# Four buffers for the powers of a latent preparation, and a new order for the steps of a cross attention and a router

## The chip, the core and the metric

The kernel runs on one NeuronCore of a Trainium2 chip. The metric is the device time of one execution in microseconds (us), as the median over runs. In the profile PE is TensorE (PEld its weight loads), DVE is VectorE, ACT is ScalarE, POOL is GpSimd and SP is the engine that here only issues transfers. One execution was also taken by the hardware profiler; all durations of single instructions come from it.

## The reference

A decoder of six blocks in float32, for x of 2 x 1024 x 256, each with a layer norm of its input and a residual. What is computed, in short:

```python
x = x + linear_attention_and_ffn(_layernorm(x))          # L0_attn
x = x + latent_attention(ctx, _layernorm(x), mask)       # L0_xattn: q, k rms-normed per head of 64
x = x + gated_cell(_layernorm(x))                        # L0_ffn: a scan of two steps
x = x + causal_attention(_layernorm(x))                  # L1_attn, 16 heads of 16
x = x + cross_attention(_layernorm(x), ctx)              # L1_xattn, 64 context rows
x = x + experts_top2(_layernorm(x))                      # L1_ffn, 8 experts, hidden 1368

def rmsnorm(x, gamma):                                   # of L0_xattn
    norm = jnp.sqrt(jnp.sum(x * x, axis=-1, keepdims=True)) * x.shape[-1] ** (-0.5)
    return x / jnp.maximum(norm, RMS_EPS) * gamma

q = (x @ wq + bq)...; k = (y @ wk + bk)...; v = (y @ wv + bv)...      # L1_xattn
attn = jax.nn.softmax(q @ k.T / 4, axis=-1)
out = (attn @ v) @ wo + bo

logits = x @ router_w                                    # L1_ffn; the two best experts of each token
hidden = gelu(expert_inputs @ w0) * (expert_inputs @ w1)
out = combine(hidden @ wo)
```

## The kernel before

x stays in SBUF as 16 tiles of 128 tokens by 256 features. The blocks run one after the other, each with pools of its own, and in most of them the order of all instructions is the order in which Python records them ("manual schedule"): each engine runs its own queue strictly in that order, and a tile of a pool is handed out again only when all that read its last content have run. A queue whose first instruction waits holds back all behind it.

Three places matter here.

**The preparation of the second batch's latents** (`Latent.prepare(1)`, called from `Latent.run` as `side`, one step between two steps of the first batch's attention). For four pairs of token tiles j it multiplies (`prod`), squares (`square`, ScalarE), keeps the product (`keep`), sums the squares per head (`sums`, VectorE, tile `p_ss` of 128x16) and raises the sums to the power of -1/2 (`inv`, L931, GpSimd, tile `p_ri`). Then come the values, and only then the four `scale` (L937, VectorE) that multiply by `p_ri`; then `qturn` and `kturn` transpose the scaled rows on TensorE (L967). The tiles `p_ss` and `p_ri` have two buffers each (`small`, `bufs=2`). The same steps for the first batch are mixed with the last steps of the block before in `JOINT_ORDER`. In the attention, additions of probabilities (`acc`, L1194) go in turn to VectorE and GpSimd, and the maxima of the scores are reduced by VectorE (`red`, L1065).

**The cross attention** (`Cross`), in four units u of 512 tokens. `CROSS_ORDER` is a list of steps written out; each word names a method and its arguments (`norm_01` is `norm(0, 1)`). For each unit: `stat`, `mean` (VectorE), `root` (a power on GpSimd, L144), `norm` (halves h of two tiles each, VectorE, through `ln_apply`, L183), `turn` (transposes), `xT` (copy from PSUM), `proj` and `q` (query, two halves c), `max` and `red` (a first pass that finds the maxima, reduced by VectorE), `part` (VectorE splits the maxima into three bfloat16 parts), `mT` and `rows` (transposes and copy of these), `sc` and `exp` (scores less the maxima, exponentials), `val`, `sum`, `inv`, `spr`, `os`, `yT` (values, divided by the sums), `out` and `add`. `bias` adds the output's bias row to x (GpSimd, L204). `text`, `keys` and `vals` prepare the context of a batch. The statistics of units 0 and 1 are computed by `stats` at the end of the block before.

Between these steps stand those of the router and the dispatch of the next block: `route_*` (a generator, `Experts.scores`, for one unit: statistics, power, norms, transposes, copy, product with the router, copy), `choose` (top two of a batch, `Experts.choose`), `ones`, `disp` and `put` (rows of the first two experts gathered by matmuls with 0/1 matrices).

PSUM has three tiles of 128x1024 ("s") and two of 128x512 ("t") in this block, so each `max`, `sc` and `spr`, which take two "s" each, waits for what read the tiles before them.

**The first expert** (`Experts.run`). `FIRST_ORDER` lists the steps that mix the first multiplications with the router of the last unit and the choice of the second batch: `up` (both input products of a slice of the hidden layer), `gelu` (ScalarE), `mul` (VectorE). Here PSUM has two "s" tiles.

Of the kernel before, what the change touches and what calls it, by code (L numbers as in the profile page):

```python
# [88 lines left out]
class Core:  # L89
# [3 lines left out]
    def __init__(self, tc):  # L93
        self.tc, self.nc, self.ps, self.tiny = tc, tc.nc, None, None
        self.turn = 0

# [22 lines left out]
    def evac(self, out, in_):  # L119

        self.turn ^= 1
        if self.turn:
            self.nc.vector.tensor_copy(out, in_)
        else:
            self.nc.scalar.copy(out, in_)

# [55 lines left out]
    def ln_apply(self, out, in_, mv, r, i):  # L182
        self.nc.vector.tensor_scalar(  # L183
            out, in_, mv[:, i, 0:1], r[:, i : i + 1], ALU.subtract, ALU.mult
        )

# [458 lines left out]
class Latent:  # L645
# [57 lines left out]
    def small(self, n, name):  # L703
        return self.pool.tile([P, n], F32, tag=name, bufs=2, name=name)
# [217 lines left out]
    def sums(self, b, j):  # L922

        nc = self.k.nc
        ss = self.of["ss", b, j] = self.small(16, "p_ss")
# [3 lines left out]
    def inv(self, b, j):  # L929
        ri = self.of["ri", b, j] = self.small(16, "p_ri")  # L930
# [850 lines left out]

CROSS_ORDER = """
text_0 stat_31 norm_00 norm_01 stat_30 turn_00 bias_0 turn_01 vals_0 text_1 keys_0 xT_0 stat_20 proj_00
vals_1 keys_1 proj_01 norm_11 stat_21 q_00 q_01 norm_10 max_01 mean_3 bias_1 mean_2 turn_11 red_010
turn_10 xT_1 red_011 root_2 proj_11 root_3 norm_21 norm_20 max_00 norm_30 bias_2 norm_31 proj_10 red_001
bias_3 red_000 q_11 q_10 part_0 max_10 turn_30 red_100 turn_31 xT_3 turn_20 red_101 turn_21 max_11 xT_2
mT_0 red_110 rows_0 red_111 sc_00 part_1 exp_00 mT_1 rows_1 sc_01 proj_21 exp_01 proj_20 sc_10 q_20 q_21
val_0 exp_10 max_20 os_0 sum_0 red_200 red_201 sc_11 inv_0 proj_30 exp_11 proj_31 max_21 q_30 q_31 sum_1
red_210 red_211 spr_0 inv_1 val_1 yT_0 part_2 os_1 out_0 spr_1 add_0 mT_2 route_stat_01 rows_2 yT_1
route_stat_00 max_30 route_mean_0 route_root_0 out_1 red_300 route_norm_01 route_norm_00 red_301  # L1790
route_turn_0 add_1 route_xT_0 route_stat_10 max_31 route_stat_11 red_311 route_prod_0 route_mean_1
red_310 route_root_1 route_copy_0 route_norm_11 sc_20 route_norm_10 part_3 route_turn_1 exp_20 mT_3
route_xT_1 sc_21 rows_3 route_prod_1 exp_21 route_copy_1 sc_31 choose_0 choose_0 sum_2 exp_31 choose_0
choose_0 inv_2 spr_2 choose_0 val_2 choose_0 os_2 yT_2 choose_0 sc_30 choose_0 out_2 exp_30 ones_03
ones_02 ones_01 ones_00 disp_00 add_2 route_stat_20 sum_3 put_00 ones_07 ones_06 ones_05 val_3 inv_3
ones_04 spr_3 os_3 route_stat_21 disp_01 yT_3 route_mean_2 put_01 out_3 route_root_2 route_norm_20
route_norm_21 add_3 route_turn_2 route_xT_2 route_prod_2 route_copy_2
# [3 lines left out]
class Cross:  # L1801
# [9 lines left out]
    def __init__(self, k, x, wt, ctxT, const):  # L1811
# [41 lines left out]
        for q in range(4):  # L1853
            part = self.to_rows[q * 32 : q * 32 + 32]
            for sign in (1, -1):
# [9 lines left out]
                for name, shape in (("mv", [P, 4, 2]), ("r", [P, 4]))]  # L1865
# [5 lines left out]
    def stats(self):  # L1871

        k, nc = self.k, self.k.nc
        for u, (mv, r) in self.early.items():
# [7 lines left out]
            yield  # L1882

# [71 lines left out]
    def root(self, u):  # L1955
        self.early[u] = self.of.pop(("mv", u)), self.k.rsqrt(self.of.pop(("ve", u)), 4)

    def norm(self, u, h):
        mv, r = self.early[u]
        xh = self.tile(u, "xh", [P, 4, D])  # L1960
        for i in self.halves(h):
            self.k.ln_apply(xh[:, i, :], self.four(u)[:, i, :], mv, r, i)

    def bias(self, u):
        self.k.add_row(self.four(u), "xb_bo")
# [10 lines left out]
    def xT(self, u):  # L1976
        xT = self.tile(u, "xT", [P, DC, 512])
        self.k.nc.scalar.copy(xT, self.of.pop(("x_s", u)).rearrange("p (c n) -> p c n", c=DC))
# [12 lines left out]
    def q(self, u, c):  # L1991
        k, s = self.k, self.of["q_s", u]
        q = self.tile(u, "q", [P, DC, 512])
        if c == 0:
            k.nc.vector.tensor_scalar(q[:, 0, :], s[:, :512], k.vec("xq_b", 0), 0.25, ALU.add, ALU.mult)
        else:
            k.nc.scalar.activation(q[:, 1, :], s[:, 512:], AF.Identity, bias=self.qb[:, 1:2], scale=0.25)
# [43 lines left out]
    def rows(self, u):  # L2041
        rows = self.tile(u, "mrows", [P, DC, 512], BF16)
        self.k.nc.scalar.copy(rows.rearrange("p c n -> p (c n)"), self.of.pop(("m_t", u)))
# [35 lines left out]
    def os(self, u):  # L2079
        os = self.tile(u, "os", [P, DC, 512])  # L2080
        self.k.nc.scalar.copy(os.rearrange("p c n -> p (c n)"), self.of.pop(("o_s", u)))
# [58 lines left out]
    def run(self, pool, moe):  # L2140
# [3 lines left out]
        nc = self.k.nc  # L2144
# [14 lines left out]
        for step in CROSS_ORDER.split():  # L2159
            name, args = step.rsplit("_", 1)  # L2160
# [7 lines left out]
            else:  # L2168
                getattr(self, name)(*args)

# [3 lines left out]
up_06 route_stat_30 up_08 gelu_06 route_stat_31 route_mean_3 mul_06 route_root_3 gelu_08 mul_08 up_04  # L2174
route_norm_30 route_norm_31 route_turn_3 gelu_04 mul_04 route_xT_3 route_prod_3 up_01 route_copy_3
choose_1 choose_1 choose_1 gelu_01 choose_1 up_00 choose_1 mul_01 choose_1 gelu_00 mul_00 up_0a choose_1
choose_1 up_05 gelu_0a ones_12 ones_13 up_07 gelu_05 ones_10 ones_11 mul_0a gelu_07 disp_10 mul_07
mul_05 up_02 put_10 ones_15 ones_16 ones_14 up_09 gelu_02 ones_17 mul_02 disp_11 gelu_09 mul_09 up_03
put_11 gelu_03 mul_03
# [3 lines left out]
class Experts:  # L2183
# [83 lines left out]
    def scores(self, u, pool, bufs=2):  # L2267
# [15 lines left out]
        yield  # L2283
        for i in range(4):
            k.ln_apply(self.xn[:, 4 * u + i, :], four[:, i, :], mv, r, i)
# [9 lines left out]
        nc.scalar.copy(xT, s.rearrange("p (c n) -> p c n", c=DC))  # L2295
# [533 lines left out]
```

## Time and profile before

| | |
|---|---|
| runs | 1703.24, 1704.68, 1713.89 us; median 1704.68 |
| profiled execution | 1704.63 us, of it 1702.8 us from the first to the last instruction (span) |
| TensorE busy | 1636.1 us, 96% of the span |
| VectorE, ScalarE, GpSimd busy | 809.1, 515.3, 310.3 us |
| mean granted TensorE clock | 0.985 |
| `prepare(1)` | statistics at 282 us, last transposes of the place at issue at 357 us |
| cross attention | from 1101.3 us (first text matmul); last routing product in it ends at 1211.4 us |
| first expert | from 1211.4 us |

All times within the execution count from the span's start. The busy share of an engine is a mean over blocks with different limits, so the prediction reads stretches of the span. "Granted clock" is the share of TensorE's full clock that the chip gave it; at 0.50 a matmul takes twice as long. In lines of the timeline the first number is the start, the second the duration in us, and the square bracket gives the idle time of the engine before it and what ended it.

### The profile page before, as it was taken

To read this page: it belongs to the slowest core of one execution; us is meant where nothing else is said; L and a number is where in the kernel's file an instruction comes from. 1 tells how busy PE (TensorE), PEld (TensorE's weight loads), DVE (VectorE), ACT (ScalarE), POOL (GpSimd) and SP (SyncE) were. 2 spreads that over 40 slices of the span, in tenths; PEclk is the share of its full clock that TensorE was granted. 3 is DMA by queue.
4 is the path that set the end of the run, shared out by engine and by line. 5 is a ranking of instruction groups with operands and counts; after the bars stand their busy time and mean duration, and the time that the engine had idled before them with its cause. 6 is when DMAs were issued, how large, how long until landed. Compare 5 with 4: busy or idle time off the path is not lost.

```text
span 1702.8 us, 21329 instructions
## 1 busy us (share of the span) xinstructions
PE 1636.1 (96%) x8816; PEld 881.5 (52%) x8822; DVE 809.1 (48%) x1458; ACT 515.3 (30%) x870; POOL 310.3 (18%) x376
## 2 busy tenths in 40 slices
PE   7999999989999999999999999889999999999998
PEld 5756544433433447333434433546785665566466
DVE  7714554465545415576667668366531311111322
ACT  2321412323233323245455455433211111111110
POOL 2003301242222202113111012220044000000520
PEclk9999999999999999989999999989899999999999
DMA  6000000000000100000000000170033322232321
GB/s 235 0 1 3 0 0 1 1 1 1 1 1 0 41 0 23 10 2 1 1 2 1 1 1 2 49 228 2 1 114 122 124 86 93 70 124 73 107 64 50
DMA packets 36824, 69.68 MB, mean 41 GB/s; under 512 B 5048, under 2 KB 28152, under 8 KB 36344
## 3 DMA queue, kind: packets, MB, share of 16 engines
q1 hardware_dynamic: 28712, 53.61, 9.4%
q0 software_dynamic: 4608, 11.54, 2.2%
q10 hardware_dynamic: 3408, 3.17, 0.5%
q8 instruction: 70, 1.15, 0.3%
q14 instruction: 26, 0.21, 0.0%
HBM read 54.15 MB, written 14.16 MB: 40 GB/s over the span
## 4 chain that ended last, share of the span: by engine, by line
PE 87%; DVE 9%; ACT 2%; issue 1%; POOL 1%; DMA 0%; SPq 0%; ACTq 0%; POOLq 0%; DVEq 0%
PE ps_s L2556 18%; PE ps_o L2583 9%; PE ps_s L1545 8%; PE ps_o L1585 5%; PE ps_s L1182 4%; PE ps_t L1504 4%; PE ps_s L1055 3%; PE ps_t L570 3%; PE ps_f L587 3%; PE ps_o L1109 3%; PE ps_t L1350 3%; PE ps_s L412 3%; PE ps_t L1620 2%; PE ps_s L904 2%; PE ps_t L1693 1%; DVE part L1561 1%
## 5 line engine op out<-in xcount | busy, mean ns | idle before, releaser
L2556 PE MATMUL ps_s<-xe,w 128*128 128x512 f32 (+1 forms) x528 | 229.0, 592 | 0.0
L1655 ACT ACTIVATE pT<-ps_t 128x512 f32<-128x512 f32 (+3 forms) x344 | 150.7, 490 | 145.3 <-PE ps_t L1620 143.1
L2571 DVE TENSOR_TENSOR hid<-ga,ps_s 128x512 f32<-128x512 f32 (+2 forms) x99 | 62.0, 628 | 268.6 <-ACT ga L2567 268.5
L1545 PE MATMUL ps_s<-kT,qT 32*128 32x512 f32 (+3 forms) x768 | 178.2, 553 | 11.2 <-DVE part L1561 7.2
L1620 PE MATMUL ps_t<-qT,kT 32*128 32x512 f32 (+3 forms) x688 | 182.0, 547 | 2.2 <-ACT pT L1655 2.2
L2556 PEld LDWEIGHTS ps_s<-xe,w 128*128 128x128 f32 (+1 forms) x528 | 98.0, 187 | 121.3 <-issue 120.0
L2583 PE MATMUL ps_o<-wo,hid 128*128 128x256 f32 (+1 forms) x704 | 153.7, 379 | 0.0
L1561 DVE TENSOR_REDUCE part<-ps_s 128x2 f32<-128x1024 f32 (+3 forms) x128 | 130.5, 1024 | 43.6 <-PE ps_t L1620 37.3
L2583 PEld LDWEIGHTS ps_o<-wo,hid 128*128 128x128 f32 (+1 forms) x704 | 133.2, 190 | 18.6 <-issue 0.5
L2567 ACT ACTIVATE ga<-ps_s 128x512 f32<-128x512 f32 (+2 forms) x99 | 54.4, 549 | 248.0 <-PE ps_s L2556 248.0
L1613 POOL TENSOR_SCALAR_AFFINE_SELECT pT<-pT 128x256 f32<-128x256 f32 x128 | 51.8, 407 | 313.5 <-ACT pT L1655 305.8
L1065 DVE TENSOR_REDUCE part<-ps_s 128x2 f32<-128x1024 f32 x64 | 77.3, 1220 | 61.0 <-PE ps_s L1055 60.4
L1545 PEld LDWEIGHTS ps_s<-kT,qT 32*128 32x128 f32 x768 | 59.9, 189 | 86.9 <-issue 43.6
L1189 ACT ACTIVATE pT<-ps_s 128x1024 f32<-128x1024 f32 x64 | 65.5, 1023 | 113.7 <-PE ps_s L1182 109.5
L1585 PE MATMUL ps_o<-pT,vr 128*32 128x256 f32 (+4 forms) x1408 | 97.9, 356 | 1.8 <-POOL pT L1613 1.5
L1553 DVE TENSOR_TENSOR ps_s<-ps_s,causal 128x256 f32<-128x256 f32 x128 | 55.0, 430 | 63.6 <-PE ps_t L1620 42.8
L2556 PE MATMUL ps_s<-xin,w 128*128 128x256 f32 (+3 forms) x264 | 83.0, 475 | 0.3 <-DVE hid L2571 0.3
L1194 POOL TENSOR_TENSOR acc<-acc,pT 128x1024 f32<-128x1024 f32 x24 | 56.3, 2347 | 146.2 <-ACT pT L1189 141.7
L1585 PEld LDWEIGHTS ps_o<-pT,vr 128*32 128x32 f32 x1408 | 28.8, 108 | 98.0 <-issue 84.1
L1620 PEld LDWEIGHTS ps_t<-qT,kT 32*128 32x128 f32 x688 | 69.8, 188 | 10.5 <-ACT pT L1655 7.0
L1055 PE MATMUL ps_s<-kT,qT 64*128 64x512 f32 x256 | 70.3, 634 | 0.8 <-DVE part L1046 0.8
L1109 PE MATMUL ps_o<-pT,vr 128*64 128x512 f32 x256 | 69.5, 624 | 0.9
(403 smaller groups left out, 2350.1 us busy)
## 6 DMA issues: line engine op xcount, KB each, us to landing
w<-in_w SPq DMA_DIRECT2D x32, 684.0 KB, 8.4
wo<-in_wo SPq DMA_DIRECT2D x8, 1280.0 KB, 7.0
xi_rows<-xin SPq DMA_DIRECT2D x8, 384.0 KB, 7.9
eo_rows<-rows ACTq DMA_DIRECT2D x12, 256.0 KB, 5.4
xr<-xi_rows POOLq DMA_DIRECT2D x48, 64.0 KB, 7.2
w_ffn<-in_w_ffn SPq DMA_DIRECT2D x1, 2304.0 KB, 14.0
x<-in_x SPq DMA_DIRECT2D x4, 512.0 KB, 5.1
w<-in_w_cell SPq DMA_DIRECT2D x2, 1024.0 KB, 16.6
```

The source lines that it names most:

```text
L1055: self.k.nc.tensor.matmul(s3[:, hh, :], lhsT=self.q[u][rows, qt * P : (qt + 1) * P], rhs=self.kt[u][rows, half * 512 : (half + 1) * 512], ...
L1065: self.k.nc.vector.tensor_reduce(self.part_of(u)[:, half, qt, :], s3, AX.X, ALU.max, negate=True)
L1109: nc.tensor.matmul(self.o[hh * 64 : hh * 64 + 64, :], lhsT=self.vr[b][:, kk, h * 64 : (h + 1) * 64], rhs=pT[:, hh, :], start=first, stop=last,
L1182: nc.tensor.matmul(s3[:, hh, :], lhsT=self.ones_h[hr, :] if i else kt[hr, kk * P : (kk + 1) * P], rhs=rows[hr, cols] if i else q[hr, cols] ...
L1504: nc.tensor.matmul(s, lhsT=self.w[name][:, kc, grp * P : (grp + 1) * P], rhs=self.xT[b][:, kc, cols], start=(kc == 0), stop=(kc == DC - 1),)
L1545: nc.tensor.matmul(s3[:, hh, :n], lhsT=q[rows, qt * P : (qt + 1) * P], rhs=kt[rows, at : at + n], start=True, stop=True,)
L1561: nc.vector.tensor_reduce(out, s3[:, :, :n], AX.X, ALU.max, negate=True)
L1585: nc.tensor.matmul(self.o[hh * 32 : hh * 32 + 32, cols], lhsT=vr[:, kk, 4 * grp + hh, :], rhs=pts[hh // 2][:, hh % 2, cols], start=first, ...
L1620: nc.tensor.matmul(out, lhsT=kt[rows, kk * P : (kk + 1) * P], rhs=q[rows, j * 512 + q0 : (j + 1) * 512], start=True, stop=True,)
L1655: nc.scalar.activation(pT[:, hh, q0:], heads[hh][:, q0:], AF.Exp)
L2556: self.k.nc.tensor.matmul(s[:m, i * 512 : i * 512 + n], lhsT=wt[:, kc, at : at + m], rhs=self.inputs[e][:, kc, first : first + n], start=( ...
L2583: self.k.nc.tensor.matmul(o, lhsT=self.hid[:n, hc, st * P : (st + 1) * P], rhs=self.to[:n, hc, :], start=(hc == 0), stop=(hc == len(HCH) - 1),
```

## The change

`p_ss` and `p_ri` get four buffers. `CROSS_ORDER` and `FIRST_ORDER` are replaced by other orders, in which a step may carry a mark ('); a marked step runs on the other engine: a marked `norm` on ScalarE instead of VectorE, a marked `xT`, `rows`, `copy` or `put` on VectorE instead of ScalarE, and a marked `q` changes its halves' engines. For a norm on ScalarE, x * r + (-mean * r), a new step `shift` computes -mean * r on VectorE (128x4). `bias` goes from GpSimd to VectorE. The router's `scores` gets the same `shift` step.

```diff
+    def copy(self, out, in_, act=True):                      # Core
+        if act != self.other:
+            self.nc.scalar.copy(out, in_)
+        else:
+            self.nc.vector.tensor_copy(out, in_)
+    def normed(self, out, in_, mv, r, shift, i):
+        if self.other:
+            self.nc.scalar.activation(
+                out, in_, AF.Identity, bias=shift[:, i : i + 1], scale=r[:, i : i + 1]
+            )
+        else:
+            self.ln_apply(out, in_, mv, r, i)
+    def shifted(self, shift, mv, r):
+        self.nc.vector.scalar_tensor_tensor(shift, mv[:, :, 0], -1.0, r, ALU.mult, ALU.mult)
...
-        ss = self.of["ss", b, j] = self.small(16, "p_ss")
+        ss = self.of["ss", b, j] = self.small(16, "p_ss", 4)
...
-        ri = self.of["ri", b, j] = self.small(16, "p_ri")
+        ri = self.of["ri", b, j] = self.small(16, "p_ri", 4)
...
 CROSS_ORDER = """
-text_0 stat_31 norm_00 norm_01 stat_30 turn_00 bias_0 turn_01 vals_0 text_1 keys_0 xT_0 stat_20 proj_00
-vals_1 keys_1 proj_01 norm_11 stat_21 q_00 q_01 norm_10 max_01 mean_3 bias_1 mean_2 turn_11 red_010
-turn_10 xT_1 red_011 root_2 proj_11 root_3 norm_21 norm_20 max_00 norm_30 bias_2 norm_31 proj_10 red_001
-bias_3 red_000 q_11 q_10 part_0 max_10 turn_30 red_100 turn_31 xT_3 turn_20 red_101 turn_21 max_11 xT_2
-mT_0 red_110 rows_0 red_111 sc_00 part_1 exp_00 mT_1 rows_1 sc_01 proj_21 exp_01 proj_20 sc_10 q_20 q_21
...
-choose_0 inv_2 spr_2 choose_0 val_2 choose_0 os_2 yT_2 choose_0 sc_30 choose_0 out_2 exp_30 ones_03
-ones_02 ones_01 ones_00 disp_00 add_2 route_stat_20 sum_3 put_00 ones_07 ones_06 ones_05 val_3 inv_3
-ones_04 spr_3 os_3 route_stat_21 disp_01 yT_3 route_mean_2 put_01 out_3 route_root_2 route_norm_20
-route_norm_21 add_3 route_turn_2 route_xT_2 route_prod_2 route_copy_2
+text_0 norm_10 norm_11' stat_31 norm_00' stat_21 turn_11 norm_01' vals_0 turn_10 keys_0 text_1 xT_1
+bias_0 proj_11 keys_1 vals_1 proj_10 bias_1 turn_01 q_10 q_11 turn_00 stat_20 max_11 xT_0 mean_2 stat_30
+root_2 proj_00 red_110 red_111 proj_01 shift_2 mean_3 norm_21' max_10 q_00 root_3 q_01 norm_20' red_101
+turn_20 red_100 turn_21 xT_2 part_1 max_00 red_000 mT_1 rows_1 red_001 max_01 shift_3 norm_31' red_010
+norm_30' red_011 sc_11 part_0 turn_30 exp_11 turn_31 xT_3' mT_0 sc_10 rows_0' bias_2 proj_20 exp_10
+bias_3 proj_21 sc_00 q_21 q_20 val_1 exp_00 os_1 max_20 sum_1 red_200 red_201 sc_01 inv_1 proj_31 exp_01
...
+rows_3' sc_31 route_copy_0 choose_0 sum_2 exp_31 val_2 inv_2 choose_0 choose_0 spr_2 os_2 choose_0 yT_2
+choose_0 choose_0 sc_30 choose_0 out_2 exp_30 choose_0 ones_00 ones_03 ones_02 sum_3 add_2 route_stat_21
+val_3 inv_3 ones_01 route_stat_20 spr_3 os_3 route_mean_2 disp_00 yT_3 route_root_2 put_00' out_3
+route_shift_2 ones_06 route_norm_21' ones_04 route_norm_20' ones_07 ones_05 route_turn_2 add_3 disp_01
+route_xT_2 route_prod_2 put_01 route_copy_2
 """
...
     def norm(self, u, h):
...
-            self.k.ln_apply(xh[:, i, :], self.four(u)[:, i, :], mv, r, i)
+            self.k.normed(xh[:, i, :], self.four(u)[:, i, :], *self.early[u], i)
     def bias(self, u):
-        self.k.add_row(self.four(u), "xb_bo")
+        four, row = self.four(u), self.k.row("xb_bo")
+        self.k.nc.vector.tensor_tensor(four, four, row.unsqueeze(1).to_broadcast([P, 4, D]), ALU.add)
...
 FIRST_ORDER = """
-up_06 route_stat_30 up_08 gelu_06 route_stat_31 route_mean_3 mul_06 route_root_3 gelu_08 mul_08 up_04
-route_norm_30 route_norm_31 route_turn_3 gelu_04 mul_04 route_xT_3 route_prod_3 up_01 route_copy_3
-choose_1 choose_1 choose_1 gelu_01 choose_1 up_00 choose_1 mul_01 choose_1 gelu_00 mul_00 up_0a choose_1
...
+route_stat_31 route_stat_30 route_mean_3 route_root_3 route_shift_3 up_0a route_norm_31 route_norm_30'
+route_turn_3 gelu_0a up_07 route_xT_3' mul_0a route_prod_3 gelu_07 mul_07 up_02 route_copy_3' choose_1
+choose_1 up_06 gelu_02 choose_1 choose_1 choose_1 gelu_06 mul_02 mul_06 up_00 choose_1 choose_1 up_03
...
```

## The prediction

> **What bounds the kernel now.** I read the page first: which engine is busy, in which slices it is not, and what the chain that ended last runs through.
>
> ```profile
> PEclk9999999999999999989999999989899999999999
> ...
> PE 87%; DVE 9%; ACT 2%; issue 1%; POOL 1%; DMA 0%; SPq 0%; ACTq 0%; POOLq 0%; DVEq 0%
> ```
>
> TensorE is the bound, with 1636.1 of 1702.8 us busy. A change that adds no matmul can win only where TensorE waits (66.7 us in all) or where its granted clock is under full (the eights). So I cut the stretches that the change touches out of the span, by windows: the latent stage around its largest wait, then the cross stage's opening (first text matmul to the last projection of the third unit), its rest, and the opening of the experts.
>
> ```profile
> 350.00:360.00 10.00, 5.00 (x18) 1.86 (x18) 7.81 (x11) 1.96 (x3) 4.79 (x2) 0.77 0.01 2
> 360.00:370.00 10.00, 10.00 (x58) 4.78 (x56) 1.27 (x2) 5.40 (x6) 6.02 (x3) 0.89 0.00 0
> 1101.30:1140.90 39.60, 32.60 (x253) 18.99 (x252) 30.58 (x64) 11.32 (x12) 11.49 (x6) 0.87 0.90 295
> 1140.90:1211.40 70.50, 65.54 (x793) 45.99 (x793) 45.88 (x117) 23.82 (x30) 3.03 (x3) 1.00 0.01 2
> 1211.40:1247.00 35.60, 34.07 (x159) 28.99 (x160) 18.38 (x73) 10.09 (x20) 1.01 (x1) 0.81 0.00 1
> ```
>
> After the window's length comes TensorE's busy time; the clock is third from the end. The opening loses 7.0 us to waits and (1 - 0.87) x 39.6 = 5.1 us to the clock; the rest 5.0 and nothing; the experts' opening 1.5 and 0.19 x 35.6 = 6.8. All of it is 25.4 us, the ceiling for everything but the first part of the change.
>
> **Four buffers in the latent preparation.** In `prepare(1)` all four `inv` stand before the first `scale`. With two buffers the third `inv` waits until `scale` has read the first result. The groups and the timeline of that place:
>
> ```profile
> L931 POOL TENSOR_TENSOR p_ri<-p_ss,minus_half 128x16 f32<-128x16 f32 x2 | 6.6, 3320 | 26.6 <-DVE qk L937 26.6
> ```
>
> ```profile
> 352.46 2.33 POOL L1194 TENSOR_TENSOR acc<-acc,pT 128x1024 f32<-128x1024 f32 x1
> 352.52 3.35 DVE L937 TENSOR_TENSOR qk<-qk,p_ri 128x1024 f32<-128x1024 f32 x1 [1.64 <-POOL p_ri L931]
> ...
> 355.93 0.69 PE L967 MATMUL ps_s<-ident,qk 128*128 128x128 f32 x2 [4.55 <-DVE qk L937]
> ```
>
> GpSimd stands still for 26.6 us, then computes both powers (6.6 us) while VectorE waits for them; the last `scale` also takes 3.35 us where others take 1.22, because a GpSimd addition (L1194) that began 0.06 us earlier holds it up; and TensorE's transposes wait 4.55 us, then 0.45 for the reduction behind.
>
> With four buffers both powers run when their sums are there (by the timeline 320.6 and 327.4), on an idle GpSimd. What is late next: the addition on GpSimd, queued behind them until now, starts when its exponential ends, at 346.8, and holds the third `scale` (VectorE is free at 348.0) until 349.2. So `scale` three and four end at 350.3 and 351.5, the reduction at 352.7, and the L1182 that began at 357.07 begins at 352.8: 4.3 us. The clock was half from about 355.4 to 362.2 (0.23 x 10 + 0.11 x 10 = 3.4 us of loss), of which some 0.5 fell into the wait: 2.9 more. Together **-7.2**; ends -4.0 (the wait goes, the clock falls anyway) and -7.5. The same two buffers in the joint order cost nothing now: there each `scale` is queued before the `inv` that needs its buffer.
>
> **Opening of the cross stage.** Here VectorE is the bound: from 1102.0 until the second `part` ends at 1133.8 it idles only 1.2 us, and TensorE's waits (2.19, 1.10, 1.57, 1.56) end on its results.
>
> ```profile
> 1112.22 2.35 POOL L204 TENSOR_TENSOR x<-x,rows 128x1024 f32<-128x1024 f32 x1 [5.38 <-DVE xh L183]
> ...
> 1112.46 2.13 DVE L1953 TENSOR_SCALAR ve<-mv 128x4 f32<-128x4 f32 x1
> ```
>
> ```profile
> L183 DVE TENSOR_SCALAR xh<-x,mv,rs_y x8: 403/407/2439, 1117.2 to 1121.5; 128x256 f32<-128x256 f32 x8
> ```
>
> The 0.17 us instruction took 2.13 because a bias addition on GpSimd ran; one norm took 2.44 instead of 0.41 for the same reason. VectorE's sum up to that `part`: 14 of 16 norm instructions go to ScalarE (four in 1.37 us, so 14 x 0.34 = -4.8); the two hold-ups go (-2.0, -2.0); two biases come (x is 128x1024 in and out, as in VectorE's L1194: 1.22 each, 1.17 following each other: +2.4; the other two biases stand behind); two `shift` (L863, 0.15: +0.3). That is -6.1. ScalarE has room: 11.3 us of 39.6 busy; its norms (four in 2.07 us at L875) add 7.3. But VectorE gets a wait of about 1.0, for the third `max`, which stands behind a projection and its copy: **-5.1**, so `part` ends at 1128.6. From there to the end of the projections (mT, two scores, two projections) it was 7.1 us, 1.5 of it clock. I laid the steps out in the new order by these durations: TensorE then waits 1.4, 0.8, 0.5, 0.6, 0.6, 1.5 and 0.5 us, and between 1120 and 1127 it has little to do, so I charge a half-clock stretch there that makes the 7.1 into 7.5. **-4.7** for the opening; ends -6.6 (clock stays up) and -1.0 (VectorE's new waits are longer).
>
> The Trainium skill has a rule that would change this (TensorE: Matmul & The Clock Gate, "HAM oscillation — how this bites in real kernels"): gaps in TensorE's work cost clock once they exceed about 3.4 us. The windows here show 0.50 for 1114 to 1118 behind a longest wait of 2.2 us, and for 1226 to 1230 behind 1.2. By the page no wait in my layout would cost clock, which is my first rival below; I go by the rows.
>
> **Rest of the cross stage.** Of its 5.0 us of waits two go: the third score no longer stands behind the copy `os` (1.13), and `disp_01` now covers the copy before `prod_2` (1.10). The others (0.3 to 0.9, for buffers that a reduction or a sum frees) come back elsewhere, at 2.6 us in my layout. What moves onto VectorE from the second `part` on (two biases 2.4, two copies of 128x1024 at 1.2, two row copies at 0.7, `put` at 0.8: 7.0) is partly paid by 12 routing norms that leave it (-4.1), and it is only 45.9 of 70.5 busy here, so I cost it at nothing; were VectorE full, up to 7 us. No transfer is added or moved, so SP's queue stays as it is, and GpSimd's only loses the four biases. **-2.3**; ends -4.5 and +2.
>
> **Opening of the experts.** This part I expect to lose. The statistics of the last routing unit wait for the router's last matmul of the unit before, then and now:
>
> ```profile
> 1211.60 1.08 DVE L2275 BATCH_NORM_STATS2 r_st<-x 128x6 f32<-128x256 f32 x3 [2.76 <-PE ps_t L2300]
> ```
>
> Before, three `up` (1.8 us each at full clock) stand between that matmul and the transposes that need the norms; now one. From that matmul's end T: statistics to T+1.9, power to T+3.4 (its row: 1213.76 to 1214.77, T being 1211.36), shift, norms: transposes from T+4.0 to T+5.3, with TensorE waiting 2.6 instead of 0. The next `up` must now wait too: its PSUM buffer is the one that the copy `xT_3` frees, and that copy, on VectorE, stands behind six small gate instructions (1.9 us): T+6.2 to T+7.4. TensorE waits another 2.15. So 4.75 us of waits against 1.5 before: +3.2. Both are followed by the routing product (128x8, little work), so the clock will fall as it did; I charge 5.1 instead of 6.8 us since one of the two dips of before, behind the copy at 1208.5, has lost its wait: -1.7. **+1.5**; ends -3.6 (no dip) and +5.
>
> **Sum.** -7.2 - 4.7 - 2.3 + 1.5 = -12.7 on the profiled execution: span 1690.1, and with the 1.8 us around it 1691.9, say **1692 us**. That execution (1704.63) stands at the median of the runs (1704.68), so nothing is to be corrected. For this kernel about 1% (17 us) is what a measurement can tell from no change.
>
> **Rivals.**
> *The clock stays up* in the new order: opening -6.6, experts +3.2 - 6.8 = -3.6, so -19.7: 1685. For it: 11.9 of the 25.4 us lost in these windows are clock, and the waits get shorter. Against: TensorE still has waits of 1.5 to 2.6 us beside matmuls of few rows or columns.
> *VectorE becomes the bound* of the whole cross stage, slower than before: the 7.0 us that move onto it stand ahead of reductions that TensorE waits for, the opening gives nothing, the experts cost +5: -7.2 + 7.0 + 5 = +4.8, 1709.4. It decides from where the stretch from the first text matmul to the last routing product grows by over 7.2 us. Against it: 24.6 us of VectorE idle in the rest.
> *The four buffers do not do it:* the freed addition on GpSimd, now at 346.8, holds the `scale` queue and TensorE gets only some 2 of the 7.2 us: -7.5, 1697. For it: the 3.35 us row. Against: only one addition falls into that place, 2.35 us long.
>
> **Chances.** Forecast 0.58, clock 0.27, VectorE 0.06, buffers 0.09. Faster by over 1% (under 1687.6): three quarters of the clock case and 0.15 of the forecast, 0.30. Slower by over 1%: 0.03, half of the VectorE case. Between: 0.67. The range reaches from somewhat beyond the clock case to the buffers case and the bad ends of the openings: 1681 to 1702.
>
> **What would show it.** Right: L967 waits under 1 us near 352 and the clock there stays 1.00; GpSimd has no wait for L937; no GpSimd bias in the opening, `ve` at 0.17; the second `part` ends 26 to 28 us after the first text matmul instead of 32.4; after the last `prod_2` TensorE waits twice, about 2.2 to 2.6 and 2.1 us. Wrong: the latent place gives less than 4 us, or the stretch from the text matmul to `prod_2` (110 us) shrinks by less than 2 or more than 12.

## The result, and the profile after

The changed kernel takes **1697.06 us** (median of 9 runs, 1690.32 to 1700.74) where the kernel before took 1709.01 beside it: a ratio of 0.9926, 95% interval 0.9899 to 0.9953, so by the ratio 12.6 us (0.74%) faster, with an interval of 8 to 17 us; the medians differ by 11.95. The changed kernel run again in another set gave 0.9926 (0.9898 to 0.9953). The profiled execution has a span of 1688.5 us, 14.3 less than before; it is the fastest of the nine, which matters below.

From the page of the changed kernel, the row of the granted clock in 40 slices, and the first rows of busy time:

```profile
PEclk9999999999999999989999999997999999999999
...
PE 1632.2 (97%) x8816; PEld 880.9 (52%) x8822; DVE 804.9 (48%) x1450; ACT 524.6 (31%) x890; POOL 300.7 (18%) x372
```

TensorE waits 1688.5 - 1632.2 = 56.3 us instead of 66.7: 10.4 of the 14.3 us are waits. The 8 of the clock in the slice from 718 us stood there before; the 7 (1140 to 1182 us) is new, and two eights of before, in the slices at 1107 and 1192 us, are gone. The same stretches as before, by windows (length, then busy time of PE, PEld, DVE, ACT, POOL, then the granted clock):

```profile
350.00:360.00 10.00, 9.06 (x49) 3.72 (x49) 6.50 (x11) 5.70 (x6) 4.66 (x2) 1.00 0.01 2
360.00:370.00 10.00, 9.16 (x58) 4.78 (x54) 6.25 (x8) 2.85 (x3) 4.68 (x2) 1.00 0.00 0
1092.70:1125.70 33.00, 28.81 (x253) 17.56 (x251) 28.91 (x58) 15.29 (x22) 2.02 (x2) 1.00 0.95 310
1125.70:1199.30 73.60, 72.67 (x794) 51.74 (x794) 44.08 (x112) 27.88 (x38) 3.02 (x3) 0.88 0.07 21
1199.30:1234.90 35.60, 31.48 (x169) 27.03 (x169) 19.71 (x77) 10.90 (x22) 1.01 (x1) 0.95 0.01 1
```

The latent place has no half clock left. The opening of the cross stage lasts 33.0 us instead of 39.6. Its rest has lost its waits (0.9 us instead of 5.0) and is nevertheless 3.1 us **longer**, because the clock there is 0.88 where it was 1.00. The opening of the experts waits more (4.1 us instead of 1.5) and lost less clock.

The latent place, by the groups of GpSimd and the timeline of that moment:

```profile
L951 POOL TENSOR_TENSOR p_ri<-p_ss,minus_half 128x16 f32<-128x16 f32 x3 | 8.7, 2899 | 9.3 <-DVE p_ss L947 9.3
```

```profile
345.89 2.34 POOL L1214 TENSOR_TENSOR acc<-acc,pT 128x1024 f32<-128x1024 f32 x1 [16.37 <-ACT pT L1209]
346.96 3.48 DVE L957 TENSOR_TENSOR qk<-qk,p_ri 128x1024 f32<-128x1024 f32 x2
...
350.50 0.44 PE L987 MATMUL ps_s<-ident,qk 128*128 128x128 f32 x2 [0.25 <-DVE qk L957]
...
351.63 1.13 PE L1202 MATMUL ps_s<-qT,kT 64*128 64x512 f32 x4 [0.69 <-DVE part L1085]
```

The powers now wait for their sums only, not for `scale` (it was 26.6 us). The freed addition on GpSimd comes at 345.9 and holds the two `scale` (3.48 us, where the two of 343.55 that met no addition took 2.35), as the prediction had it; TensorE's wait is 0.25 instead of 4.55, and the next one, for the reduction, 0.69 instead of 0.45.

The opening of the experts, by the timeline:

```profile
1203.31 1.47 PE L2325 MATMUL ps_s<-ident,w 128*128 128x128 f32 x8 [2.14 <-DVE w L191]
...
1206.22 3.52 PE L2591 MATMUL ps_s<-xin,w 128*128 128x256 f32 x8 [1.44 <-DVE xT L133]
```

Both forecast waits are there, the first at 2.14 (forecast 2.2 to 2.6), the second at 1.44 (forecast 2.15).

### The profile page after: what moved, and what is told of

Read it like the earlier page. It is cut to its first block, busy times and chain, and to the rows that moved or that the text cites. A ratio compares the mean times of both kernels' runs of the same rounds, so it can differ in the third digit from the quotient of the medians.

```text
span 1688.5 us, 21340 instructions
## 1 busy us (share of the span) xinstructions
PE 1632.2 (97%) x8816; PEld 880.9 (52%) x8822; DVE 804.9 (48%) x1450; ACT 524.6 (31%) x890; POOL 300.7 (18%) x372
## 5 line engine op out<-in xcount | busy, mean ns | idle before, releaser
L2606 DVE TENSOR_TENSOR hid<-ga,ps_s 128x512 f32<-128x512 f32 (+3 forms) x99 | 62.1, 628 | 267.1 <-ACT ga L2602 267.0
L1565 PE MATMUL ps_s<-kT,qT 32*128 32x512 f32 (+3 forms) x768 | 177.7, 551 | 11.1 <-DVE part L1581 7.1
L2602 ACT ACTIVATE ga<-ps_s 128x512 f32<-128x512 f32 (+3 forms) x99 | 54.4, 549 | 249.1 <-PE ps_s L2591 249.0
L2591 PE MATMUL ps_s<-xin,w 128*128 128x256 f32 (+3 forms) x264 | 79.0, 459 | 1.9 <-DVE xT L133 1.4
L1640 PEld LDWEIGHTS ps_t<-qT,kT 32*128 32x128 f32 x688 | 69.8, 188 | 10.9 <-ACT pT L1675 7.0
## 6 DMA issues: line engine op xcount, KB each, us to landing
w_ffn<-in_w_ffn SPq DMA_DIRECT2D x1, 2304.0 KB, 13.9
```

The source lines that it names most:

```text
L1565: nc.tensor.matmul(s3[:, hh, :n], lhsT=q[rows, qt * P : (qt + 1) * P], rhs=kt[rows, at : at + n], start=True, stop=True,)
L1640: nc.tensor.matmul(out, lhsT=kt[rows, kk * P : (kk + 1) * P], rhs=q[rows, j * 512 + q0 : (j + 1) * 512], start=True, stop=True,)
L2591: self.k.nc.tensor.matmul(s[:m, i * 512 : i * 512 + n], lhsT=wt[:, kc, at : at + m], rhs=self.inputs[e][:, kc, first : first + n], start=( ...
L2606: self.k.nc.vector.tensor_mul(self.hid[:m, hc, first : first + n], self.act.pop(hc)[:m, :n], self.now.pop(hc)[:m, 512 : 512 + n])
```

## The experiments

In the set of the first four (four buffers, four for `p_ri`, two buffers, GpSimd bias) every kernel took some 22 us more, the kernel before too (1731.28): their profiles show TensorE waiting 17 to 18 us in the first expert, while GpSimd scatters the tokens, which it does in the other profiles without such waits; why is not known. Their ratios are to the kernel before of the same set, in which the changed kernel itself was not run, so they meet its 0.9926 across sets; their stretches end ahead of that place. In the table the stretches are those of the one profiled execution: when the first text matmul begins, from there to the third unit's last projection (opening), to the third routing product's end (rest), to the fourth's, and from the text matmul to the end of the span.

| kernel | ratio to before (95%) | text at | opening | rest | to 4th product | text to end |
|---|---|---|---|---|---|---|
| before | | 1101.3 | 39.5 | 70.6 | 11.7 | 601.5 |
| changed | 0.9926 (0.9899 to 0.9953) | 1092.7 | 33.0 | 73.6 | 12.2 | 595.8 |
| changed, again | 0.9926 (0.9898 to 0.9953) | 1100.2 | 34.7 | 70.7 | 13.8 | 598.9 |
| before + four buffers | 0.9972 (0.9952 to 0.9993) | 1103.6 | 39.5 | 70.6 | 11.7 | |
| before + four for p_ri | 0.9958 (0.9932 to 0.9983) | 1094.3 | 39.2 | 72.9 | 12.4 | |
| changed, two buffers | 0.9975 (0.9949 to 1.0001) | 1099.4 | 33.0 | 72.0 | 13.8 | |
| changed, GpSimd bias | 0.9972 (0.9949 to 0.9995) | 1093.1 | 36.0 | 72.0 | 13.9 | |
| before + VectorE bias | 1.0021 (0.9996 to 1.0047) | 1109.4 | 42.7 | 70.6 | 10.2 | 598.7 |
| changed, VectorE norms | 0.9976 (0.9948 to 1.0004) | 1101.6 | 38.7 | 72.9 | 13.8 | 605.3 |
| changed, other opening order | 0.9939 (0.9912 to 0.9966) | 1099.4 | 35.7 | 72.1 | 10.9 | 596.8 |
| changed + 2 fills | 0.9922 (0.9894 to 0.9951) | 1094.4 | 35.7 | 68.4 | 12.1 | 593.2 |
| both of these | 0.9911 (0.9880 to 0.9942) | 1099.0 | 34.0 | 68.4 | 10.9 | 591.4 |
| changed + 7 fills | 0.9912 (0.9879 to 0.9944) | 1099.7 | 34.6 | 68.4 | 11.1 | 591.0 |
| 7 fills, GpSimd bias | 0.9897 (0.9869 to 0.9926) | 1095.6 | 35.7 | 68.4 | 11.1 | 592.1 |

### The four buffers alone

```
-        return self.pool.tile([P, n], F32, tag=name, bufs=2, name=name)
+        return self.pool.tile([P, n], F32, tag=name, bufs=bufs, name=name)
-        ss = self.of["ss", b, j] = self.small(16, "p_ss")
+        ss = self.of["ss", b, j] = self.small(16, "p_ss", 4)
-        ri = self.of["ri", b, j] = self.small(16, "p_ri")
+        ri = self.of["ri", b, j] = self.small(16, "p_ri", 4)
```

> The kernel before with four buffers for both powers and sums, and nothing else. My theory (the buffers alone bring the latent part of the gain): TensorE's wait before the transposes at L967 falls from 4.55 us to under 0.5, the half-clock stretch at 355 is gone, and cross's first text matmul comes at 1092.7 us instead of 1101.3 (-8.6, as in the changed kernel). Span of the profiled execution some 1694, unless the clock falls elsewhere behind that place; ratio to before 0.995. Rival (the freed GpSimd addition holds VectorE, the rest of the 8.6 comes from somewhere else): the text matmul at 1097 or later, -4.5 at most.

The second variant leaves `p_ss` at two:

> The kernel before with four buffers for the powers (p_ri) alone; the sums (p_ss) keep two. My theory: only the powers' buffer holds anything up, since a power that runs early frees its sum early; so it is the same as with both (text matmul at 1092.7 within 0.5 us). Rival: the third sum waits on the first power, which delays the chain, and half or more of the 8.6 us is missing (text matmul at 1097 or later).

At the place itself both do the whole: L1182, at 357.07 before, begins at 352.20 and 352.38, with waits of 0.25 and 0.24 us at L967, and the half clock at 355 is gone. The powers' buffer alone was the cause. Yet one of the two reaches the cross stage 2.3 us *later* than the kernel before and the other 7.1 earlier. By windows of the stages between (first the kernel with both buffers, then the one with `p_ri` alone):

```profile
340.00:370.00 30.00, 27.93 (x152) 12.25 (x148) 21.61 (x25) 11.77 (x12) 11.69 (x5) 1.00 0.00 1
500.00:820.00 320.00, 301.26 (x1567) 146.26 (x1567) 163.76 (x285) 113.14 (x202) 59.91 (x72) 0.93 0.03 10
```

```profile
500.00:820.00 320.00, 300.07 (x1629) 145.36 (x1632) 168.78 (x289) 115.15 (x206) 60.59 (x74) 0.97 0.03 10
```

The same code, which the two kernels reach within 0.2 us of each other, had a clock of 0.93 in one and 0.97 in the other; 0.04 x 320 is 13 us, nearly twice the gain that was being looked for. The kernel before has 0.97 there, the changed kernel 0.96, and 0.93 when it was run again. So the 2.3 us later are no sign for the rival, although they are what it forecast: with `p_ri` alone, where the clock behind the place is that of the kernel before, the text matmul comes 7.1 us earlier. A single span says little about a change of 5 us, and the ratio over many runs counts: 0.9972 and 0.9958, or 4.8 and 7.3 us.

### The cross stage and the experts alone

This is the changed kernel with both `small(16, ..., 4)` back at two.

> The changed kernel with two buffers for the powers and sums again: the cross stage and the opening of the experts alone. If the parts add up, the wait of some 4.5 us at L987 and the half-clock stretch at 355 are back, the text matmul is at 1101.3, and the span is that of the changed kernel plus 8.6: 1697. Two theories on the 17 us of half clock behind the routing products (1158.7 to 1175.8 in the changed kernel): if the kind of work there causes it, it stays behind the same products, with all else 8.6 us later (1167 to 1184); if the phase of the work against the clock's own windows causes it, another shift moves or removes it, and the rest of the cross stage takes 65 instead of 73.6 us.

```profile
354.86 0.69 PE L987 MATMUL ps_s<-ident,qk 128*128 128x128 f32 x2 [4.55 <-DVE qk L957]
```

The wait is back, and the ratio 0.9975 is 4.3 us; with the 4.8 to 7.3 of the buffers that makes 9 to 11.6 of the 12.6: the parts add up within their intervals, which are wide (0.9975 reaches to 1.0001). The half clock behind the routing products stayed with them although the phase was another: rest 72.0, where the changed kernel's would be 73.6 x 0.88 = 65 at full clock. That speaks for the kind of work; its length varies from one execution to the next.

### The biases

Back on GpSimd in the new order, and onto VectorE in the old one:

```
-        four, row = self.four(u), self.k.row("xb_bo")
-        self.k.nc.vector.tensor_tensor(four, four, row.unsqueeze(1).to_broadcast([P, 4, D]), ALU.add)
+        self.k.add_row(self.four(u), "xb_bo")
```

> The changed kernel with the biases of the cross stage back on GpSimd, in the new order. My theory (a GpSimd addition of 128x1024 holds VectorE up for about 2 us when they meet, so it costs VectorE more than the 1.2 us of doing it itself): the instructions of VectorE that meet the first two additions take 2 us longer, and the opening (first text matmul to the last projection of the third unit, 32.9 us in the changed kernel) takes 34 to 36. Rival (GpSimd's addition is work taken off VectorE): 2.4 us less on VectorE, the opening takes 31 or less.

> The kernel before, in its own order, with the biases of the cross stage on VectorE instead of GpSimd, and nothing else. The prediction's term: two hold-ups of 2.0 us go and 2.4 us of VectorE work come, so the second part on VectorE ends 1.6 us earlier than 32.4 us behind the first text matmul, at 30.8. Rival, after the run with the biases back on GpSimd (opening 2 us shorter at full clock): VectorE loses by doing them itself, also in the old order; the second part ends at 33 to 35. In both, instructions such as ve (2.13 us before) take their 0.17 us again. The span moves by less than 3 us either way, plus what the clock does.

In the new order GpSimd's additions do hold VectorE's casts up. Timeline of the changed kernel with them (its later casts take 0.31 to 0.33):

```profile
1110.13 2.35 POOL L224 TENSOR_TENSOR x<-x,rows 128x1024 f32<-128x1024 f32 x1 [2.15 <-ACT xh L198]
```

```profile
1111.13 1.53 DVE L2054 CAST mparts<-m 128x64 bf16<-128x64 f32 x1
...
1119.16 1.73 DVE L2054 CAST mparts<-m 128x64 bf16<-128x64 f32 x1
```

The second `part` ends 29.1 us behind the text matmul instead of 27.4, and the opening takes 36.0; but (1 - 0.86) x 36.0 = 5.0 of these are half clock (by its window) that the changed kernel did not have there in its first profile; in its second, with one such stretch, it has the biases on VectorE and the second `part` at 29.1 as well. The ratio 0.9972 does not price the bias either: by mean span times mean granted clock, the clock took 50 us of this kernel's runs and 39 of the runs of the kernel before in that set. The last pair of experiments, without half clock in either opening, prices the bias alone: the second `part` at 30.0 us with it on GpSimd against 27.9, the opening 35.7 against 34.6, so 1.1 us in favour of VectorE; over the runs the pair cannot be told apart.

In the old order it is the other way round. `ve` takes 0.17 us again, as predicted; and yet the second `part` ends at 35.4 us behind the text matmul instead of 32.4 (forecast 30.8), and the ratio is 1.0021 (0.9996 to 1.0047), so no gain. The forecast of 30.8 counted two additions, as in the new order; in the old order all four stand ahead of the second `part` (VectorE takes them at 1113.06, 1121.77, 1127.59 and 1131.88), 4.8 us of work against the 4.0 of the two hold-ups, and VectorE's waits for the maxima grow from 1.2 to 3.5 us. The rival's outcome holds there. In this kernel the move shortens the opening only in the order that leaves two of the additions until behind it.

### All norms on VectorE

The marks (`'`) are taken off the 13 `norm` steps of `CROSS_ORDER`.

> The changed kernel with all norms of cross and routing on VectorE again, in the new order. The prediction's term: norms on ScalarE took 4.8 us off VectorE in the opening. If VectorE still sets the opening there, the stretch from the first text matmul to the third unit's last projection grows from 33.0 us (35.7 with two short half-clock stretches) to 37 to 40. Rival: with the new order VectorE has room for them, and the stretch stays within 1.5 us of 33.0 to 35.7; the norms for ScalarE were then not needed.

Windows of the opening:

```profile
1101.60:1140.30 38.70, 31.89 (x253) 19.10 (x251) 33.12 (x72) 9.19 (x10) 2.11 (x2) 0.91 0.92 301
```

38.7 us, within the forecast of the theory, though (1 - 0.91) x 38.7 = 3.5 of them are half clock, where the changed kernel lost none in one profile and (1 - 0.95) x 34.7 = 1.7 in the other. VectorE has 14 instructions more and 33.12 instead of 28.91 us of work: 4.2 us, 0.30 each (predicted 0.34 and 4.8), and its second `part` ends 33.1 us behind the text matmul instead of 27.4 and 29.1. The ratio goes from 0.9926 to 0.9976 (0.9948 to 1.0004): without the shared norms a gain can no longer be told from none. By mean span times mean clock this kernel still saves 7.5 us where the changed one saves 9, and its loss of clock is 3 us above that of the kernel before; so part of what the norms cost comes through the clock.

### Another order at the opening of the experts

```
+up_06 route_stat_30 up_08 gelu_06 route_stat_31 route_mean_3 mul_06 route_root_3 gelu_08 mul_08 route_shift_3 up_04
+route_norm_30 route_norm_31 route_turn_3 gelu_04 mul_04 route_xT_3 up_01 route_prod_3 gelu_01 mul_01 route_copy_3
+choose_1 choose_1 choose_1 choose_1 up_00 choose_1 choose_1 gelu_00 mul_00 up_0a choose_1
...
```

> The changed kernel with another order at the opening of the experts: three hidden products (up) stand before the transposes of the last routing unit, as in the kernel before, and one more between the transposes and the routing product. My theory (the new opening order costs TensorE about 3.6 us of waits, and the clock behind them): the waits of 2.1 and 1.4 us go, no half-clock stretch follows the last routing product, and the time from the third to the fourth routing product's end is 10.5 us or less where the changed kernel had 12.3 and its two variants with other buffers or biases 13.8 and 13.9; with what the clock loses behind it, 4 to 9 us less than the changed kernel on the same chip. Rival (the experts' stage is set by something behind, such as the scatter of the tokens, so that its opening is free): the stretch is shorter but the span stays within 2 us of the changed kernel's.

```profile
1211.45 1.99 PE L2591 MATMUL ps_s<-xin,w 128*128 128x256 f32 x8 [0.71 <-DVE hid L2606]
...
1219.62 0.41 PE L2372 MATMUL ps_t<-m,strict 128*128 128x32 f32 x2 [1.56 <-DVE m L2361]
...
1231.14 1.99 PE L2591 MATMUL ps_s<-xin,w 128*128 128x256 f32 x8 [1.62 <-DVE hid L2606]
```

The two waits of 2.14 and 1.44 went and three others make up for them, 3.89 us for the 4.08 of before (the two and one of 0.50): all three end on VectorE, whose queue holds the statistics, norms and choice. A half-clock stretch came all the same, 3.4 us from 1220.5. The fourth product ends earlier (10.9 us), but the ratio, 0.9939, is no better. My theory fell. The rival's outcome came, a shorter stretch and a time that cannot be told from the changed kernel's, but not for the reason it names: what took the gain back in the profile are these waits, not the scatter.

### What makes the clock fall

The new loss of clock was the largest thing the prediction did not have. Windows of the changed kernel, cut at the clock's own steps (in each of the fourteen profiles all changes of the clock lie on one grid of 3.41 us):

```profile
1155.27:1158.68 3.41, 3.02 (x46) 2.54 (x44) 3.27 (x10) 2.23 (x5) 1.01 (x1) 1.00 0.02 5
1158.68:1162.09 3.41, 3.41 (x18) 3.08 (x19) 2.89 (x8) 1.14 (x4) 0.00 (x0) 0.51 0.00 0
...
1165.51:1168.92 3.41, 3.41 (x23) 3.41 (x21) 0.69 (x1) 1.67 (x2) 0.00 (x0) 0.50 0.00 0
...
1172.34:1175.75 3.41, 3.41 (x68) 3.15 (x69) 0.00 (x0) 2.08 (x3) 0.00 (x0) 0.50 0.02 5
```

TensorE is busy for all of it and the clock stays at half. What is busy are routing products of 128x8 and scores with 32 rows. In the second profile of the same kernel the clock falls at 1170.1 us behind a window in which TensorE is busy for all 3.41 us.

So I gave each matmul record of the profiles the share of the array that it uses (rows/128 x columns/128) times its elements at 1.14 per ns (a 128x512 record with all rows and columns takes 0.45 us), and summed that over each 3.41 us. Of the 6740 windows in the fourteen profiles (their first 30 us and what lies behind 1680 us left out), 255 come out under 0.40, and 231 of these are followed by a window of half clock; of the 6485 above it 15 are.

TensorE's busy time alone separates worse: of the 6494 windows at full clock 116 are followed by a fall, and the best bound on the share misjudges 22 windows, the best bound on busy time 49. (Rows alone misjudge 25, so what the columns add is not shown.) That is a fit to these traces, and the bound of 0.40 is no more than that. The test: add full matmuls that nobody needs (in `scores`, `xT` being the unit's rows, into the PSUM tile that the product overwrites):

```
         t = k.t()
+        if u < 2:
+            for kc in range(DC):
+                nc.tensor.matmul(t, lhsT=k.ident, rhs=xT[:, kc, :], start=(kc == 0), stop=(kc == DC - 1))
```

> The changed kernel with useless work added: ahead of the routing products of units 0 and 1 two matmuls of 128x512 with 128 rows, into the same PSUM tile, which the products then overwrite. They cost 2 x 1.0 us at full clock. Theory A (the half clock behind these products comes from matmuls that keep TensorE busy but use few rows and columns of it: 128x8 outputs, 32 rows): the 13.7 to 17.1 us of half clock between the routing products go, so the stretch from the first text matmul to the third routing product's end shrinks from 105.0 to 108.0 us to 101 to 103, although work was added: 4 to 6 us faster than the changed kernel. Theory B (the clock falls because of the short waits there, or by chance of the phase): the waits stay, the half clock stays, and the stretch grows by 2 us, or by 4 at half clock.

```profile
1130.10:1198.50 68.40, 67.46 (x802) 47.59 (x802) 44.08 (x112) 27.87 (x38) 3.02 (x3) 1.00 0.04 13
```

More work (two pairs of 1.8 us each, not 1.0 as I had put it), the same waits (0.94 us), and the stretch is 68.4 us, at a clock of 1.00, where the changed kernel's two profiles have 73.6 and 70.7. It is not one lucky execution: in all six profiles of the new order without these fills half clock follows the routing products (10.2 to 17.1 us), and in all four with them none does. Theory A is shown for this place, theory B is out. Over the runs it gives 0.9922 against 0.9926, so nothing that can be told apart: the fills cost much of what they bring.

> The two variants together: the added matmuls ahead of the first two routing products and the other order at the opening of the experts. If both theories hold they add up: 8 to 13 us less than the changed kernel on the same chip, ratio to the kernel before some 0.985. If the opening of the experts or the clock is given back later, less than 4.

0.9911, some 2.6 us under the changed kernel by the ratios and far from the 8 to 13: the other opening order brought nothing to add, and the fills little.

The control, the changed kernel again:

> The changed kernel itself once more, as a measure for the others on this chip. If its gain stands on any chip: ratio to before 0.990 to 0.995. Theory on the clock: the half-clock stretch behind the routing products of units 0 and 1 is there again (13 to 17 us long), the one at the opening of the experts too, at 3.4 to 13.7 us, since the first comes from the kind of work and the second from where its windows fall. Rival: without the same phase both are gone, and the stretch from the first text matmul to the third routing product is 100 us or less.

Windows of its rest and of its opening of the experts:

```profile
1134.80:1205.50 70.70, 69.76 (x794) 48.98 (x794) 44.04 (x112) 27.87 (x38) 3.02 (x3) 0.93 0.05 16
1205.50:1241.10 35.60, 31.49 (x144) 26.56 (x144) 18.72 (x73) 9.74 (x19) 1.01 (x1) 0.81 0.00 1
```

The half clock behind the products is there again, at 10.2 us shorter than the 13 to 17 I expected, and the one at the experts is long (13.7 us); its profiled span is 1699.0 where the first was 1688.5. Ahead of the text matmul alone the same program lost 7.4 us more.

### Fills at every dip, and the best version

```
+        if (u, c) == (1, 1):                                    # max
+            self.k.fill(pair[0][:, :512], self.of["xT", u])
...
+        if u < 2:                                               # mT
+            self.k.fill(t, self.of["xT", u])
...
+        if u == 3:                                              # scores, ahead of the transposes
+            for h in range(2):
+                k.fill(s[:, :512], self.x[:, 12:16, :].rearrange("p (h i) d -> p h (i d)", h=2))
```

> The changed kernel with useless work at every place of cross and of the experts' opening where the half clock began: pairs of 128x512 matmuls with 128 rows, one ahead of the scores of unit 1 whose q TensorE waits 1.76 us for, one ahead of the two transposes of part 0 and 1 (waits of up to 0.8), one ahead of each of the first two routing products, two ahead of the last routing unit's transposes (2.1 us of wait). Some 7 us of work, 4 of them inside waits. Theory A (too few rows and columns in work for some 3.4 us make the clock half): no half clock from the first text matmul to 30 us behind the fourth routing product, where the changed kernel had 17.1 + 3.4 in one execution and 3.4 + 10.2 + 13.7 in another; 3 to 9 us faster than the changed kernel. Theory B: the added 3 us show and the clock falls all the same: slower than the changed kernel.

> The same with the biases back on GpSimd. The run with the biases on GpSimd alone had an opening 2 us shorter but for the clock. If the added matmuls hold the clock up there: 2 us faster than the variant with the added matmuls alone, and the fastest of all, some 8 us under the changed kernel. If GpSimd's additions hold VectorE up instead, or the clock falls at another place of the opening: the same or slower.

Windows of the three stretches with the seven fills:

```profile
1099.70:1134.30 34.60, 33.08 (x265) 19.37 (x264) 28.97 (x58) 15.09 (x22) 2.02 (x2) 1.00 0.95 310
1134.30:1202.70 68.40, 67.46 (x801) 47.59 (x802) 44.08 (x112) 27.87 (x38) 3.02 (x3) 1.00 0.05 15
1202.70:1238.30 35.60, 33.79 (x183) 28.39 (x182) 20.64 (x82) 11.29 (x23) 1.61 (x2) 1.00 0.00 1
```

No half clock in any, with 12.6 us of useless work in them: 591.0 us from the text matmul to the end instead of 595.8 and 598.9. With the biases on GpSimd it is 592.1, so the 2 us I expected of that are not there. Over the runs the two have 0.9912 and **0.9897** (median 1689.34). The second is the fastest kernel of the study, ahead of the changed one by some 5 us by the ratios; the intervals overlap, and the two cannot be told from each other. Estimated by mean span times mean clock, its whole gain over the kernel before is clock: its runs have 1675.4 us at full clock and 12.7 us lost to it, those of the kernel before 1674.3 and 32.1.

## Why the prediction was right

The forecast was 1692 us on the profiled execution, -12.7; the ratio over the runs says -12.6 (-8 to -17), the profiled span -14.3, and a second profiled execution of the same program only -3.8. (In absolute terms the runs have 1697 us, beside 1709 and not 1705 for the kernel before.) That forecast and ratio agree to 0.1 us is luck: in the first profile the four terms miss by 1.4 to 5.3 us, in both directions, and cancel. What was right is the mechanism in two of the four places, the buffers and VectorE's work in the opening. Step by step:

- **Four buffers, -7.2.** Right. From the matmuls ahead of it the place took 4.5 us less until L1182 began (forecast 4.3), and the half clock at 355 with its 3.4 us of loss is gone (forecast 2.9 beyond the wait). Alone the buffers bring 4.8 and 7.3 by the ratios. The rival with the held-up `scale` had the mechanism and not the size.
- **Opening of cross, -4.7.** Right: -6.5 in one execution, -4.9 in the other, as no half clock or one step of it falls there. The second `part` ends at 27.4 us in the first, inside the forecast 26 to 28, and at 29.1 in the second. The norms were rightly sized (4.2 for 4.8). The bias term, -4.0 + 2.4, holds in the new order only: 2.1 us at the second `part` and 1.1 of the opening, where 1.6 was counted; in the old order, with four additions ahead, the second `part` comes 3 us later. One reading of the trace was wrong: of the four waits of TensorE that were said to end on VectorE's results, two (2.19 and 1.10) end on ScalarE's `q` and `xT`.
- **Rest of cross, -2.3.** Wrong: +3.0 and +0.1. The waits fell by 4.1, more than the 2.4 of the layout, but I charged no clock, and behind the routing products it cost (1 - 0.88) x 73.6 = 8.8 us in one execution and (1 - 0.93) x 70.7 = 4.9 in the other. The failed step is "-2.3; ends -4.5 and +2": it looked for what TensorE waits for, and this loss is in work.
- **Opening of the experts, +1.5.** The two waits were forecast at 4.75 and were 3.6, the same in both executions. For the clock 5.1 us were charged; it cost (1 - 0.95) x 35.6 = 1.8 in the first profile and (1 - 0.81) x 35.6 = 6.8 in the second. Together with all behind it this part came to -2.2 us in the first and +2.2 in the second; the forecast lies between them, which one profile could not have told.

The rival with the clock that stays up (-19.7) was met by neither profile (-14.3 and -3.8): the clock falls differently in each execution. By all runs of the second set, mean span times mean clock, an estimate of the time at full clock, is 1705.2 x 0.9838 = 1677.6 before and 1694.3 x 0.9847 = 1668.4 after: 9 of the 11 us are not clock, and the loss of clock is 28 and 26 us, nearly the same. In the first profile the change took 8.5 us of that loss away at the latents and in the opening (3.4 and 5.1) and added 8.8 behind the routing products. VectorE as the bound of the whole stage is refuted: 110.2 us from the text matmul to the third product became 105.4 to 106.6.

The Trainium skill (TensorE: Matmul & The Clock Gate, "HAM oscillation — how this bites in real kernels") speaks of gaps over about 3.4 us; in this case the clock fell with TensorE busy for 3.02 of the 3.41 us ahead, in another execution for all of them, and stayed down with it busy all the time. So the prediction was right to go by the rows, and its rows (waits of 1.2 to 2.2 us) were still too narrow a reason.

## What to carry to other kernels

Read a stretch of half clock by what TensorE does in it, not only by what it waits for: in this kernel matmuls with few rows or few moved elements (32 rows; 128x8 outputs) did little to hold the clock up, and two such steps side by side, or one beside a wait, halved the clock of what followed until denser work came. When an operation moves off a shared resource, count what then stands ahead of the critical step in the order at hand: the biases on VectorE shortened the opening by 1.1 us in the order with two of them ahead of the second `part`, and made that `part` 3 us later in the order with four. And where one program's spans differ by 10 us, judge a part of the change by its own stretch and by the ratio of many runs, not by one span.

## What the runs showed of the hardware

- Half clock tends to last: at half clock the same matmuls move half the elements per 3.41 us (the 128x8 records start 0.21 us apart instead of 0.11), so by the share used above work that held full clock before need not bring it back. In the stretch behind the routing products the windows come to 0.28 to 0.42; it lasted until the 64 matmuls of `sum` (last of the windows shown, 3.41 us with 68 matmuls), which bring theirs to 0.54.
- Useless matmuls can pay within a stretch: 3.6 us of them made 70.7 to 73.6 us into 68.4. Over whole runs two pairs gave nothing that can be told (0.9922 against 0.9926).
- The same program lost 22 to 39 us of 1700 to the clock from run to run (mean clock 0.977 to 0.987), with nothing else different; that fits work which falls on other places of the clock's steps of 3.41 us, but what shifts it from run to run was not tried.
- A GpSimd addition of 128x1024 stretched casts on VectorE from 0.32 to 1.53 and 1.73 us, though these touch another tile.
